# A long convolution by nine block products instead of ten, with the sums for it on POOL

## The chip, the cores and the metric

The kernel runs on one core of a Trainium2 chip. The core has a matrix engine (TensorE, PE in the profile, with its weight loads as PEld), a vector engine (DVE), a scalar engine (ACT), a general engine (POOL) and a queue that issues transfers (SP); POOL issues indirect transfers of its own. Each engine works through its own instructions in a fixed order and waits on semaphores for the others. The metric is the device time of one execution in microseconds (us), the median of several runs. Four runs of the kernel before took 3074.35, 3076.90, 3073.13 and 3070.82 us, with a median of 3073.74 us.

## The reference, cut to what matters

The program is two layers of a network (a convolution with gates, a mixture of experts, an attention, a feed-forward part). The change concerns the first of them alone, for `x` of shape (16, 256, 512) and a context `ctx` of the same shape:

```python
vr  = v.reshape(B, 32, 8, 512)              # v = layernorm(x); x2 = x1 = ctx
kv  = vr[:, :, :, None, :] * x2r[:, :, None, :, :]        # B, 32, i, j, 512
y   = irfft(rfft(kv, 1024) * rfft(k, 1024))[..., :512]    # causal convolution, one filter k[h] per h
y   = y + kv * skip
out = einsum('bhijl,bhil->bhjl', y, x1r)
```

So for each of 32 filters (h), 16 batches and 8 x 8 pairs (i, j), a sequence of 512 products is convolved with a filter of 512 taps, weighed by the context and summed over i. The first expert layer that follows uses weights `w1` and `w2` of eight experts, 4 MB each.

## The kernel before, in words

The convolution is done as matrix products with a Toeplitz matrix. The 512 positions are cut into four blocks of 128. Write x0 to x3 for the four blocks of `kv`, and T0 to T3 for the four 128x128 blocks of the Toeplitz matrix of one filter (`ut`, loaded per filter from `in_kt`). Then block l of the result is the sum over m up to l of T(l-m) x(m): one product for block 0, two for block 1, three for block 2 and four for block 3, ten in all. Each product has 128x128 weights and 512 columns, and the profile counts two passes for each in fp32.

The loop of `conv_shared` (L744) runs over the 32 filters h. A step h has two halves of eight batches, so that 8 batches x 64 pairs give the 512 columns. `conv` (L283) does one half: for each block lc, the products on PE (L292), then on DVE the weighing by the context (L297, out of PSUM into `pr`) and the sum over i (L304, into one block of `oT`), and then one of the four products `kv` of the half after it (`product`, L274, on DVE). `extra` puts small pieces of other work between them. Around the two halves of a step stand, in this order on PE: the transposes of the step before (`norm2_turned`), the list `mid`, the turning of the next step's inputs (`turn_inputs`: `pvt`, `pt`, `psk`, L256 to L262), half 1, the keys (`keys`, L211), the list `end`, and four transposes of `oT` (`after_conv`, L316, tile `po`), one for each block. DVE then adds `po` to `xt` (L317), and statistics on DVE (L78, L80), four small operations on POOL (L82 to L86) and one on ACT (L91) make the normalized rows `xh`. `begin(h + 2)` does the same statistics for the inputs of a later step, between the keys and `end`.

`mid` and `end` carry the shared expert and the router of the four steps before, and differ with q = h % 4, so that four steps make a group:

- q = 0: `mid` holds one `outs` (L503) and the router's `parts` (L396); `end` holds a short `whole` (L407).
- q = 1: `mid` one `hidden` (L490), `end` `rank_rows` and one `hidden`; the router's `tops` lies between the blocks on DVE, and its exponential (L439) on ACT in half 1.
- q = 2: `mid` one `hidden`, `end` one `hidden`; here POOL sends twelve indirect transfers of a group in a row (L371 to `xgd`, L1910 to `rtok`).
- q = 3: `mid` one `outs`, `end` two; each `outs` ends in an addition on DVE (L507).

In steps 3 to 18 `ranks` (L663, L667, L668, on DVE, and two indirect transfers to `tokd` on POOL) stands behind `end` and ahead of `after_conv`; steps 0, 2 and 22 have other pieces of the sorting there.

What sets the order: PE, DVE and ACT keep the order in which the code is written (`manual_schedule`, L743). POOL's and SP's order is chosen by the scheduler when the kernel is built and then fixed. Three PSUM buffers `y` take turns (`ps_y`), `pvt` has one, `kv` two, `ut` two, `ct` three. The expert weights are loaded one quarter per step by SP from step 2 on, four quarters of `w1` and then four of `w2` (`load_experts`, L339, the last one in step 9); the first product with `w2` comes after the loop (L914).

Of the kernel before, what the change touches and what calls it, by code (L numbers as in the profile page):

```python
# [42 lines left out]
class Kernel:  # L43
# [59 lines left out]
    def conv_shared(self, x1d, xgd):  # L103
        nc, tc, a = self.nc, self.tc, self.a
        with ExitStack() as ctx:
# [136 lines left out]
            def begin(h):  # L242

                xt, ct, ut = loaded.pop(h)
                vh = hp.tile([P, D], F32, tag="vh", name="vh")
                self.normalized(vh, xt, self.stats(xt, small))
                return {"h": h, "xt": xt, "ct": ct, "ut": ut, "vh": vh, "kv": {}}

            def skipped(c):

# [2 lines left out]
                nc.vector.scalar_tensor_tensor(z, c["vh"], skip[:, h : h + 1], c["ct"], ALU.mult, ALU.mult)  # L253

            def turn_inputs(c):
                c["vt"] = vt = ps_v.tile([P, DC, P], F32, tag="v", name="pvt")  # L256
                for k in range(DC):
                    nc.tensor.transpose(vt[:, k, :], c["vh"][:, k * P : (k + 1) * P], self.ident)
# [10 lines left out]
            def product(c, half, mc):  # L269

                cols = slice(half * 64, half * 64 + 64)
                if mc == 0:
                    c["kv"][half] = hp.tile([P, DC, hb * NH * NH], F32, tag="kv", name="kv")
                nc.vector.tensor_tensor(  # L274
                    c["kv"][half][:, mc, :].rearrange("p (b j i) -> p b j i", i=NH, j=NH),
                    c["vt"][:, mc, cols].rearrange("p (b i) -> p b i", i=NH)
                    .unsqueeze(2).to_broadcast([P, hb, NH, NH]),
                    c["cT"][:, mc, cols].rearrange("p (b j) -> p b j", j=NH)
                    .unsqueeze(3).to_broadcast([P, hb, NH, NH]),
                    ALU.mult,  # L280
                )

            def conv(c, half, nxt, extra):  # L283

                cols = slice(half * 64, half * 64 + 64)
                if half == 0:
                    c["oT"] = hp.tile([P, DC, P], F32, tag="oT", name="oT")
                kv, ut, cT = c["kv"].pop(half), c["ut"], c["cT"]
                for lc in range(DC):
                    y = ps_y.tile([P, hb * NH * NH], F32, tag="y", name="y")  # L290
                    for mc in range(lc + 1):
                        c["conv"] = nc.tensor.matmul(  # L292
                            y, ut[:, (lc - mc) * P : (lc - mc + 1) * P], kv[:, mc, :],
                            start=(mc == 0), stop=(mc == lc),
                        ).ins
                    pr = hp.tile([P, hb, NH, NH], F32, tag="pr", name="pr")
                    nc.vector.tensor_tensor(  # L297
                        pr,
                        y.rearrange("p (b j i) -> p b j i", i=NH, j=NH),
                        cT[:, lc, cols].rearrange("p (b i) -> p b i", i=NH)  # L300
                        .unsqueeze(2).to_broadcast([P, hb, NH, NH]),
                        ALU.mult,
                    )
                    nc.vector.tensor_reduce(  # L304
                        c["oT"][:, lc, cols].rearrange("p (b j) -> p b j", j=NH), pr, AX.X, ALU.add
                    )
                    if nxt is not None:
                        product(*nxt, lc)
                    for f in extra.get(lc, []):
                        f()  # L310

            def after_conv(c):
                xt = c["xt"]
                po = ps_t.tile([P, DC, P], F32, tag="t", name="po")
                for lc in range(DC):
# [23 lines left out]
            def load_experts(c):  # L339
                if c < DC:  # L340
                    nc.sync.dma_start(
                        self.e_w1[:, c].rearrange("p (e h) -> p e h", h=EH),
                        a["w1"].rearrange("e (c p) h -> c p e h", p=P)[c],
                    )
                else:
                    c -= DC
                    n = E * EH // P // 4
                    nc.sync.dma_start(
                        self.e_w2.rearrange("p (f d) -> p f d", d=D)[:, n * c : n * c + n, :],
                        a["w2"].rearrange("e (c p) d -> p (e c) d", p=P)[:, n * c : n * c + n, :],  # L350
                    )

            xhs = []

# [388 lines left out]
            with tc.manual_schedule(engines=order):  # L743
                for h in range(HC):  # L744
# [9 lines left out]
                    with tc.issue_after(last_load[0]):  # L754
                        if w is None:
                            w = load_shared_weights()
                        if 2 <= h < 2 + DC + 4:
                            load_experts(h - 2)
                    now["w"] = w
                    now["xt"].append(c["xt"])  # L760
# [59 lines left out]
                    if last:  # L820
                        with tc.issue_after(self.normed):
                            for t in range(T4 - 1):
                                send(now["r"], t)
                    turn = (now["xT"], h)
            norm2_turned(*turn)
            r = logits(now, T4 - 1, 1)
            for f in tops(r):
# [12 lines left out]
                send_route(r, 0)  # L840
            for t in range(T4):
                outs(now, t)


    def routed(self, xgd, ygd, early):
# [1241 lines left out]
```

## Time and profile before

| what | value |
|---|---|
| median of four runs | 3073.74 us (3070.82 to 3076.90) |
| the profiled execution: time, span | 3076.3 us, 3074.6 us |
| PE busy, share of the span | 3002.9 us, 98% |
| DVE, ACT, POOL busy | 1434.3, 661.7, 923.1 us |
| from 35 to 960 us (the convolution): PE, DVE, ACT, POOL busy of 925 us | 900.64, 677.73, 148.14, 291.37 us |
| the Toeplitz products, L292 (1280 passes, all in the convolution) | 565.7 us |

Times in the profile are microseconds from the span's start. A group's row gives the line, the engine, the operation, the tiles out and in, the number of instructions, the busy time and the mean of one in ns, and then the idle time of that engine just before them with what ended it. Matmuls overlap, so 1280 passes with a mean of 592 to 597 ns each start 0.429 us apart (20 passes of one half from 493.80 to 502.38 us). In a timeline a row gives the start, the duration and the instruction; brackets hold the idle time before it and what released it. A chain of waits names who waited for whom, the sum, the number of times and the longest.

### The profile page before, as it was taken

How to read it: one execution, taken by the hardware profiler on the slowest of the kernel's cores; microseconds unless marked ns; L12 is line 12 of the kernel's file. 1: busy time of each engine (PE TensorE's matmuls, PEld its weight loads, DVE VectorE, ACT ScalarE, POOL GpSimd, SP SyncE). 2: the span in 40 equal slices, each digit the busy share in tenths (PEclk: the TensorE clock that was granted, in tenths of full speed). 3: DMA queues.
4: the chain of work that ended last, by engine and by line, in shares of the span. 5: the costliest groups of instructions: out<-in, count | busy, mean ns of one | idle time of the engine just before them, and what ended most of it. 6: DMA issues, size and time to landing. Idle time of an engine off the chain costs nothing.

```text
span 3074.6 us, 34728 instructions
## 1 busy us (share of the span) xinstructions
PE 3002.9 (98%) x12825; PEld 1529.8 (50%) x12825; DVE 1434.3 (47%) x2652; ACT 661.7 (22%) x1250; POOL 923.1 (30%) x1270
## 2 busy tenths in 40 slices
PE   8999999999999999889999999999999999999998
PEld 4444444445455666554554554454444444444443
DVE  6777777777664434443433333443333232222222
ACT  1111111111111111243333323324121111111110
POOL 2233333232223200165545555534110300301201
PEclk9999999999999999989999999999999999999999
DMA  4232211211215653311211221212120100100100
GB/s 118 70 104 88 63 60 56 71 57 60 59 39 182 204 168 129 109 55 46 87 52 52 76 64 47 69 53 69 59 103 28 55 14 14 55 10 11 45 0 29
DMA packets 119218, 209.87 MB, mean 68 GB/s; under 512 B 27592, under 2 KB 47976, under 8 KB 118400
## 3 DMA queue, kind: packets, MB, share of 16 engines
q1 hardware_dynamic: 90752, 125.63, 13.4%
q0 software_dynamic: 28288, 81.92, 8.2%
q8 instruction: 105, 1.72, 0.2%
q14 instruction: 73, 0.60, 0.1%
HBM read 140.12 MB, written 67.37 MB: 67 GB/s over the span
## 4 chain that ended last, share of the span: by engine, by line
PE 85%; DVE 6%; issue 5%; POOL 3%; DMA 1%; ACT 0%; SPq 0%; POOLq 0%; DVEq 0%; ACTq 0%
PE y L292 15%; PE po L1879 14%; PE ph L1821 13%; PE po L1625 9%; PE phg L895 4%; PE pog L914 4%; PE pqn L1504 3%; PE pout L503 3%; PE ph L490 3%; PE pqr L1501 2%; PE pqn L1512 2%; PE pt L99 2%; PE pqr L1508 1%; DVE pr L297 1%; PE ptg L884 1%
## 5 line engine op out<-in xcount | busy, mean ns | idle before, releaser
L292 PE MATMUL y<-kv,ut 128*128 128x512 f32 x1280 | 565.7, 597 | 0.6 <-DVE pr L297 0.6
L1625 PE MATMUL po<-nw,w 128*128 128x512 f32 x1024 | 445.7, 593 | 0.0
L1879 PE MATMUL po<-p,ht 128*128 128x512 f32 x1024 | 445.1, 592 | 0.0
L292 PEld LDWEIGHTS y<-kv,ut 128*128 128x128 f32 x1280 | 243.2, 192 | 297.3 <-issue 287.1
L1625 PEld LDWEIGHTS po<-nw,w 128*128 128x128 f32 x1024 | 192.0, 190 | 235.1 <-issue 229.6
L1879 PEld LDWEIGHTS po<-p,ht 128*128 128x128 f32 x1024 | 192.7, 190 | 233.4 <-issue 232.0
L1821 PE MATMUL ph<-w,w 128*128 128x512 f32 x640 | 281.2, 592 | 0.0
L297 DVE TENSOR_TENSOR pr<-y,cT 128x512 f32<-128x512 f32 x256 | 174.5, 682 | 145.2 <-PE y L292 145.1
L1883 DVE TENSOR_TENSOR res<-res,po 128x512 f32<-128x512 f32 x128 | 87.7, 685 | 315.5 <-PE po L1879 315.5
L1821 PEld LDWEIGHTS ph<-w,w 128*128 128x128 f32 x640 | 121.5, 190 | 152.6 <-issue 152.6
L304 DVE TENSOR_REDUCE oT<-pr 128x64 f32<-128x512 f32 x256 | 175.6, 686 | 8.8
L274 DVE TENSOR_TENSOR kv<-pvt,cT 128x512 f32<-128x512 f32 x256 | 173.9, 680 | 0.0
L1919 POOL DMA_INDIRECT gw<-kvd,keys_of x128 | 133.5, 1043 | 49.8 <-issue 37.8
L267 POOL TENSOR_TENSOR xt<-xt,sk 128x512 f32<-128x512 f32 x32 | 40.8, 1274 | 339.8 <-DVE sk L266 281.9
L1519 DVE TENSOR_TENSOR w<-pqr,w 128x512 f32<-128x512 f32 (+1 forms) x72 | 45.4, 631 | 202.7 <-ACT sw L1517 189.0
L895 PE MATMUL phg<-w,xTg 128*128 x568 | 134.5, 380 | 0.6 <-issue 0.5
L914 PE MATMUL pog<-w,hT 128*128 x284 | 133.6, 593 | 0.0
L1504 PE MATMUL pqn<-w,m 128*128 128x512 f32 (+1 forms) x288 | 116.9, 548 | 7.2 <-ACT kn L1537 7.2
L490 PE MATMUL ph<-xT,w_s 128*128 128x512 f32 x256 | 117.5, 603 | 0.0
L1821 PE MATMUL ph<-xT,w 128*128 128x512 f32 x256 | 116.4, 592 | 0.0
L503 PE MATMUL pout<-w_s,ht 128*128 128x512 f32 x256 | 115.3, 600 | 0.0
L1835 ACT ACTIVATE ht<-ht,p1b 128x512 f32<-128x512 f32 x96 | 69.3, 722 | 212.9 <-DVE ht L1840 212.9
(291 smaller groups left out, 3771.8 us busy)
## 6 DMA issues: line engine op xcount, KB each, us to landing
xg<-xgd SPq DMA_DIRECT2D x71, 256.0 KB, 2.8
ygd<-y SPq DMA_DIRECT2D x71, 256.0 KB, 2.0
xt<-in_x_dram SPq DMA_DIRECT2D x32, 256.0 KB, 3.4
ct<-in_ctx_dram SPq DMA_DIRECT2D x32, 256.0 KB, 3.3
ut<-in_kt_dram SPq DMA_DIRECT2D x32, 256.0 KB, 2.6
w<-in_w_dram SPq DMA_DIRECT2D x8, 1024.0 KB, 5.3
x1d<-xt SPq DMA_DIRECT2D x32, 256.0 KB, 2.9
x3s<-xt POOLq DMA_DIRECT2D x32, 256.0 KB, 2.8
```

The lines of the kernel that those rows point to most:

```text
L274: nc.vector.tensor_tensor(c["kv"][half][:, mc, :].rearrange("p (b j i) -> p b j i", i=NH, j=NH), c["vt"][:, mc, cols].rearrange("p (b i) - ...
L292: c["conv"] = nc.tensor.matmul(y, ut[:, (lc - mc) * P : (lc - mc + 1) * P], kv[:, mc, :], start=(mc == 0), stop=(mc == lc),).ins
L297: nc.vector.tensor_tensor(pr, y.rearrange("p (b j i) -> p b j i", i=NH, j=NH), cT[:, lc, cols].rearrange("p (b i) -> p b i", i=NH) .unsque ...
L304: nc.vector.tensor_reduce(c["oT"][:, lc, cols].rearrange("p (b j) -> p b j", j=NH), pr, AX.X, ALU.add)
L490: nc.tensor.matmul(ph, w["sw1"][:, c, f * P : (f + 1) * P], xT[:, c, :], start=(c == 0), stop=(c == DC - 1),)
L503: nc.tensor.matmul(po, st["ht"][f][:, tok], w["sw2"][:, f, :], start=(f == 0), stop=(f == NC_ - 1))
L895: nc.tensor.matmul(ph, xT[:, c, :], w1[:, c, bass.ds(e * EH, EH)], start=(c == 0), stop=(c == DC - 1))
L914: nc.tensor.matmul(po, hT[:, q, :], w2[:, bass.ds(e * (EH * D // P) + q * D, D)], start=(q == 0), stop=(q == EH // P - 1),)
L1504: nc.tensor.matmul(pqn[k][i], m0[:, 2 * hp + i, :], q0, start=True, stop=False)
L1625: nc.tensor.matmul(po, ut[:, n].rearrange("p a j q -> p (a j q)"), nw[:, 2 * hp + i, :], start=(n == 0), stop=(n == HEADS - 1),)
L1821: nc.tensor.matmul(ph, w[:, c, :], x[:, c, :], start=(start and c == 0), stop=(c == half - 1), skip_group_check=True,)
L1879: nc.tensor.matmul(po, ht[f, i // T4][:, toks], w2[:, f, :], start=(f == fs[0]), stop=(f == fs[-1]))
```

## The change

Block 2 and block 3 share a product. With s = x0 + x1,

- block 2 = T2 s + (T1 - T2) x1 + T0 x2
- block 3 = T2 s + (T3 - T2) x0 + T1 x2 + T0 x3

which is nine products, where T2 s counts once. New work makes the operands and takes the shared product apart:

- `differences`: two 128x128 subtractions on POOL per step, T1 - T2 and T3 - T2 (`dt`).
- in `product`, once two of the four blocks of a half are there, one 128x512 addition on POOL (`x01`, the sum s).
- in `conv`, the product T2 s goes to a PSUM buffer `m`; ACT copies it to SBUF (`both`); three products of block 3 go to a `y` buffer; DVE adds them onto `both`; POOL multiplies `both` by the context (before, DVE did this for all four blocks). Then two more products add onto `m` for block 2, and DVE weighs and sums block 2 as before. The sum over i of block 3, on DVE, is kept back as `late`: it stands after block 1's sum of the next half, or, for half 1, at the head of `after_conv`.
- the order of a half is now block 0, block 1, T2 s, block 3, the rest of block 2. `y` has two PSUM buffers and `m` one.
- `sums`, `twice` (`both`) and `diffs` lie in the last quarter of `w2`'s place in SBUF; so the load of this quarter is moved from step 9 to behind the loop (`load_second(3)`).

```diff
             def turn_inputs(c):
+                differences(c)
...
+                if mc == 1:
+                    c["sum"][half] = x01 = sums[half]
+                    nc.gpsimd.tensor_tensor(x01, c["kv"][half][:, 0, :], c["kv"][half][:, 1, :], ALU.add)
+            mixed = lambda lo, n: self.e_w2[:, E * EH * D // P - lo - n : E * EH * D // P - lo]
+            sums, twice, diffs = [mixed(i * D, D) for i in range(2)], mixed(2 * D, D), [
+                mixed(3 * D + i * 2 * P, 2 * P).rearrange("p (i x) -> p i x", i=2) for i in range(2)
+            ]
+            def differences(c):
+                c["dt"] = dt = diffs[c["h"] % 2]
+                ut = c["ut"].rearrange("p (d x) -> p d x", x=P)
+                for i in range(2):
+                    nc.gpsimd.tensor_tensor(dt[:, i, :], ut[:, 2 * i + 1, :], ut[:, 2, :], ALU.subtract)
...
-                for lc in range(DC):
-                    y = ps_y.tile([P, hb * NH * NH], F32, tag="y", name="y")
-                    for mc in range(lc + 1):
-                        c["conv"] = nc.tensor.matmul(
-                            y, ut[:, (lc - mc) * P : (lc - mc + 1) * P], kv[:, mc, :],
...
+                products(y, [(T[0], x[0])])
+                weighed(0, y)
+                if nxt is not None:
+                    product(*nxt, 0)
+                beside(0)
+                y = block("y", 2)
+                products(y, [(T[1], x[0]), (T[0], x[1])])
+                weighed(1, y)
+                if "late" in c:
+                    c.pop("late")()
+                for k in (1, 2):
+                    if nxt is not None:
+                        product(*nxt, k)
+                    beside(k)
+                y2 = block("m", 1)
+                products(y2, [(T[2], x01)])
+                both = twice
+                nc.scalar.copy(both, y2)
+                y = block("y", 2)
+                products(y, [(dt[:, 1, :], x[0]), (T[1], x[2]), (T[0], x[3])])
+                nc.vector.tensor_tensor(both, both, y, ALU.add)
+                nc.gpsimd.tensor_tensor(by_i(both), by_i(both), ctx_(3), ALU.mult)
+                if nxt is not None:
+                    product(*nxt, 3)
+                beside(3)
+                products(y2, [(dt[:, 0, :], x[1]), (T[0], x[2])], start=False)
+                weighed(2, y2)
+                c["late"] = lambda: summed(3, by_i(both))
 
             def after_conv(c):
+                c.pop("late")()
                 xt = c["xt"]
...
-                        if 2 <= h < 2 + DC + 4:
+                        if 2 <= h < 2 + DC + 3:
                             load_experts(h - 2)
...
                     turn = (now["xT"], h)
+            self.load_second(3)
             norm2_turned(*turn)
```

`weighed(lc, y)` is the weighing out of PSUM followed by `summed`, the sum over i; `beside(k)` runs the small pieces that stood behind block k.

More of the change, by code (lines that the diff above doesn't have):

```diff
@@ L246, in begin @@
                 self.normalized(vh, xt, self.stats(xt, small))
-                return {"h": h, "xt": xt, "ct": ct, "ut": ut, "vh": vh, "kv": {}}
+                return {"h": h, "xt": xt, "ct": ct, "ut": ut, "vh": vh, "kv": {}, "sum": {}}
             def skipped(c):
@@ L288, in conv, with products, summed @@
                 kv, ut, cT = c["kv"].pop(half), c["ut"], c["cT"]
-                for lc in range(DC):
-                    y = ps_y.tile([P, hb * NH * NH], F32, tag="y", name="y")
-                    for mc in range(lc + 1):
+                x01, dt = c["sum"].pop(half), c["dt"]
+                T = [ut[:, d * P : (d + 1) * P] for d in range(DC)]
+                x = [kv[:, m, :] for m in range(DC)]
+                by_i = lambda t: t.rearrange("p (b j i) -> p b j i", i=NH, j=NH)
+                ctx_ = lambda lc: (
+                    cT[:, lc, cols].rearrange("p (b i) -> p b i", i=NH).unsqueeze(2).to_broadcast([P, hb, NH, NH])
+                )
+                def products(y, terms, start=True, stop=True):
+                    for k, (t, v) in enumerate(terms):
                         c["conv"] = nc.tensor.matmul(
-                            y, ut[:, (lc - mc) * P : (lc - mc + 1) * P], kv[:, mc, :],
-                            start=(mc == 0), stop=(mc == lc),
+                            y, t, v, start=(start and k == 0), stop=(k == len(terms) - 1), skip_group_check=True
                         ).ins
[L296 to L303, printed above, removed]
+                def summed(lc, pr):
                     nc.vector.tensor_reduce(
@@ L306, in conv, with weighed, beside @@
                     )
-                    if nxt is not None:
-                        product(*nxt, lc)
-                    for f in extra.get(lc, []):
-                        f()
+                def weighed(lc, y):
+                    pr = hp.tile([P, hb, NH, NH], F32, tag="pr", name="pr")
+                    nc.vector.tensor_tensor(pr, by_i(y), ctx_(lc), ALU.mult)
+                    summed(lc, pr)
+                def beside(k):
+                    for f in extra.get(k, []):
+                        f()
+                block = lambda tag, bufs: ps_y.tile([P, hb * NH * NH], F32, tag=tag, name=tag, bufs=bufs)
+                y = block("y", 2)
[10 more added lines that the diff above has]
+                for k in (1, 2):
+                    if nxt is not None:
+                        product(*nxt, k)
[4 more added lines that the diff above has]
+                nc.scalar.copy(both, y2)
+                y = block("y", 2)
+                products(y, [(dt[:, 1, :], x[0]), (T[1], x[2]), (T[0], x[3])])
[7 more added lines that the diff above has]
+                c["late"] = lambda: summed(3, by_i(both))
             def after_conv(c):
+                c.pop("late")()
                 xt = c["xt"]
@@ L345, in load_experts @@
                 else:
[L346 to L351, printed above, removed]
+                    self.load_second(c - DC)
             xhs = []
@@ L842, in conv_shared, with load_second @@
                 outs(now, t)
+    def load_second(self, c):
+        n = E * EH // P // 4
+        self.nc.sync.dma_start(
+            self.e_w2.rearrange("p (f d) -> p f d", d=D)[:, n * c : n * c + n, :],
+            self.a["w2"].rearrange("e (c p) d -> p (e c) d", p=P)[:, n * c : n * c + n, :],
+        )
     def routed(self, xgd, ygd, early):
```

## The prediction

> **What bounds the kernel now.** First the page: span, engines, the group of the changed line.
>
> ```profile
> span 3074.6 us, 34728 instructions
> ...
> PE 3002.9 (98%) x12825; PEld 1529.8 (50%) x12825; DVE 1434.3 (47%) x2652; ACT 661.7 (22%) x1250; POOL 923.1 (30%) x1270
> ...
> L292 PE MATMUL y<-kv,ut 128*128 128x512 f32 x1280 | 565.7, 597 | 0.6 <-DVE pr L297 0.6
> ...
> L267 POOL TENSOR_TENSOR xt<-xt,sk 128x512 f32<-128x512 f32 x32 | 40.8, 1274 | 339.8 <-DVE sk L266 281.9
> ```
>
> PE is the bound, and its Toeplitz passes waited 0.6 us in all: each pass removed is time, unless PE must wait where it didn't. Next PE's chain of waits up to 1000 us, whose first row is nearly all of it:
>
> ```profile
> PE pvt L258 <- DVE kv L274: 17.2, 11, 3.6
> ```
>
> Then the end of a half 1, where the change puts a DVE sum ahead of PE's transposes: the timelines of DVE and PE at step 16 (q = 0).
>
> ```profile
> 493.33 0.64 PE L316 MATMUL po<-ident,oT 128*128 128x128 f32 x4
> ```
>
> ```profile
> 492.14 0.69 DVE L304 TENSOR_REDUCE oT<-pr 128x64 f32<-128x512 f32 x1
> 492.75 0.68 DVE L274 TENSOR_TENSOR kv<-pvt,cT 128x512 f32<-128x512 f32 x1
> 493.34 0.68 DVE L78 BATCH_NORM_STATS2 ln_st<-xt 128x6 f32<-128x512 f32 x1
> 494.13 0.18 DVE L80 BATCH_NORM_AGGREGATE ln_mv<-ln_st 128x2 f32<-128x6 f32 x1
> 494.23 0.77 DVE L663 TENSOR_TENSOR cmp<-o_krow,o_key 128x512 f32<-128x512 f32 x1
> 495.03 0.69 DVE L667 TENSOR_REDUCE o_rank<-cmp 128x2 f32<-128x512 f32 x1
> 495.75 0.23 DVE L668 TENSOR_SCALAR o_where<-o_rank,o_batch 128x2 int32<-128x2 f32 x1
> 495.89 0.68 DVE L317 TENSOR_TENSOR xt<-xt,po 128x512 f32<-128x512 f32 x1
> ```
>
> PE transposes `oT` at 493.33 because its last sum ended at 492.83; DVE comes to `after_conv` only at 495.89. That lag costs nothing today. Last, POOL in step 18 (q = 2), where twelve indirect transfers, 1.275 us apart, fill it:
>
> ```profile
> 529.59 1.04 POOL L371 DMA_INDIRECT xgd<-xh,slots  x1 [1.56 <-DVE slots L466]
> ...
> 543.73 0.97 POOL L1910 DMA_INDIRECT rtok<-rt,o_where  x1 [0.30 <-issue]
> 544.71 1.30 POOL L267 TENSOR_TENSOR xt<-xt,sk 128x512 f32<-128x512 f32 x1
> 549.03 0.32 POOL L216 TENSOR_TENSOR kr<-kr,tab 128x64 f32<-128x64 f32 x1 [3.02 <-ACT kr L215]
> ```
>
> **A. Removed: 64 products.** 64 halves x 2 passes x 0.429 us (20 passes from 493.80 to 502.38) = -54.9 us, all on PE's path.
>
> **B. Removed: PE's waits for `kv`.** `pvt` waits for the fourth `kv` of half 0. That product now stands ahead of block 2's weighing and sum, and DVE starts closer behind PE (see C): in step 17 DVE would end it about 11.4 us after PE's transposes, and PE arrive at 12.0. I take all 17.2 us: -17.2.
>
> **Work beside.** DVE keeps 12 operations of 0.68 us per half (the addition onto `both` takes the place of one weighing). ACT gains a copy, 0.586 us (a 128x512 copy out of PSUM, L100) x 64 = 37.5 us; POOL 128 operations of 1.27 us and 64 of 0.455 us (L225, 128x128), 192 us on 291 of 925. On average there is room; what counts is who waits.
>
> **C. Added: the late sum ahead of `po`.** DVE reaches it after `begin`'s statistics, `end`'s additions and `ranks`. In half 1 DVE's new list is about as long as PE's 7.72 us, so block 2's weighing starts right behind PE, as the last one did before; only the `kv` product (0.60 us from start to start) is no longer behind it, and the late sum (0.69) comes in. So the sum ends about where L317 could start today, + 0.1 us. The first three transposes don't wait, which gives back 3 x 0.11. From each step's rows: q = 0 with `ranks` (4, 8, 12, 16) 2.4 us each, without (20, 24, 28) 0.8; q = 3, where L507 waits for PE first and the 0.69 comes in full, 2.8 with `ranks` (7, 11, 15) and 1.25 without (19, 23, 27); q = 1 none (PE is busy longer); steps 1, 2, 3: 1.5, 4.0, 3.2; step 31: 1.1. In q = 2 it is POOL that is late: in the order as built, the sum s of half 1 and both context products lie among and behind the twelve transfers: 529.6 + 12 x 1.275 + 4 x 1.27 + 1.3 = 551.3 less the last gap 0.3 = 551.0; late sum 551.1 to 551.8; PE arrives at 550.1: 1.4 x 7. Sum: 9.7 + 2.3 + 8.5 + 3.7 + 8.8 + 1.1 + 9.9 = +44.0 us. DVE's queue behind it (L317, statistics) moves with it.
>
> **D. Added: PE waits for ACT's copy** before block 2's last two products, 6.0 us into a half. The copy stands behind what ACT still holds. q = 1, half 1: behind the exponential.
>
> ```profile
> 515.60 0.15 DVE L438 TENSOR_TENSOR ex<-m,m 128x4 f32<-128x4 f32 x1
> ```
>
> That half began at 510.10; with the late sum ahead, `ex` leaves DVE 6.2 us into the half, ACT's 0.21 and 0.59 follow: PE goes on at 7.2: 1.2 x 7 = 8.4. The half 0 behind a q = 2 step with `ranks`: POOL, free at 551.0, does keys, statistics, both differences (0.91 more) and two `tokd` transfers before `xh`; ACT's `xh` ends near 560.0, the copy at 560.6, PE wants it at 551.9 + 0.4 + 6.0 = 558.3: 2.35 x 4 = 9.4. Behind a q = 0 step with `ranks`: 0.65 x 4 = 2.6. Elsewhere the copy is in time. Sum +20.4.
>
> **E. The start.** POOL's first difference waits for `ut`, ahead of the first `vh`, which PE waits for (8.50 us): two of 0.455 and a wait for the load, together 0.9 to 2.5; I take +1.8.
>
> **F. Restarts.** No row shows a pass behind a wait inside a group; between 0 (weights already in) and 0.19 us (the L292 weight load). 39 waits come and 11 go: 0 to 5.3; I take 5.3, since at `pvt` the weight loads waited too.
>
> **G. The clock.** After the 1.89 us pause ending at 390.28 the granted clock fell; after an equal one in step 17 it didn't:
>
> ```profile
> 389.00:394.00 5.00, 3.72 (x12) 2.14 (x13) 1.22 (x2) 1.98 (x3) 0.00 (x0) 0.75 0.01 3
> 505.00:510.00 5.00, 3.11 (x14) 1.67 (x13) 3.05 (x10) 1.25 (x2) 0.00 (x0) 1.00 0.00 0
> ```
>
> (the fraction behind POOL's count is the clock). It cost 1.7 us (step 13 took 32.23 us, others of its kind 30.54); the 3.59 us pause in step 3 cost 3.2. So one pause in five near 1.9 us trips it, a long one surely. Of my new pauses of 2.3 us and more I let nine half-rate stretches follow: 9 x 1.7 = 15.3, less 4.9 that go, less 2.0 where a slow PE waits less in D: +8.4; bounds -4.9 and +25. The Trainium skill ("TensorE: Matmul & The Clock Gate", HAM oscillation) warns only of idle gaps above some 3.4 us; by it one or two of mine would trip, G would be an estimated -2, and the sum some 10 us lower; the 1.89 us row speaks against it.
>
> **The moved load.** One 1 MB transfer (0.43 us on SP, 5.3 us to land) leaves step 9, where nobody waited, and stands behind the loop after an `x1d` store near 936 us; `e_b` and two stores queue behind it. The first product with `w2` is at 977: 0, covered by 35 us; without that cover 5.3 and the store ahead.
>
> **Sum.** -54.9 - 17.2 + 44.0 + 20.4 + 1.8 + 5.3 + 8.4 = +7.8 on the profiled 3076.3 us gives 3084.1. That run stands 2.6 above the median, so 3081.5 us, 0.25% slower.
>
> **Unknown prices.** POOL's context product reads an operand with repeats: 1.27 (L267, plain, same size) to 1.82 us (four times L225, which repeats). POOL's rows of 32, 64 and 128 elements (253, 321, 455 ns) lie on one line, which gives 1.26 at 512: 1.27 taken; 1.82 adds some 12 us in q = 2. Sharing between POOL and DVE: none to see in 513.90 to 515.17, where DVE kept 0.69 and 0.68; 0 taken. ACT's copy 0.59 to 0.81 (L91).
>
> **The rivals.**
> 1. *Faster: the late sum is not waited for* (chance 0.17). If DVE gains on PE inside half 1, it reaches the sum before PE reaches the fourth transpose, and C falls, with half of F and G: 3081.5 - 44 - 7 = 3030, and up to 3062 where only the waits under 2 us vanish. Deciding point: DVE 2.5 us earlier at step 16's 495.89. For: PE leaves DVE idle 145 us before L297. Against: that idle time lies inside the halves, while the eight rows above run without a gap.
> 2. *POOL binds in more steps* (0.15): its products take 1.8 us or wait behind its transfers. C and D grow by 12 to 25: 3094 to 3107. Against: 484 of 925 us busy.
> 3. *Every new pause of a microsecond or more trips the clock* (0.08): 25 stretches, G +37 at most: 3098 to 3110.
> 4. *The late load collides* with `e_b` and the expert rows (0.05): 5 to 10 us, 3087 to 3092.
>
> **How the numbers follow.** My case has 0.55, with a range of 3064 to 3098 (D and C each a third off). Within it I put 0.28 slower, 0.17 the same, 0.10 faster; 0.2% (6 us) is about what this kernel's runs can tell from nothing. Rival 1 is faster; 2, 3 and 4 slower, but for 0.01. Faster 0.27, same 0.18, slower 0.55. The range of 8 in 10 leaves out two thirds of rival 1 and the top of 2 and 3: 3052 to 3106.
>
> **What would show it.** L292's successor with 1152 passes near 509 us and 0.429 us apart (A); no `pvt` wait on `kv` (B); a new first row, `po` waiting for DVE `oT`, 24 times and near 44 us, longest near 4 (C); block 2's passes waiting for ACT, 15 times and 20 us (D); more stretches under full clock before 960 us (G). It is wrong if `po` waits under 20 us, or if POOL's 128x512 operations run above 1.4 us.

## The result, and the profile after

The changed kernel takes 3077.12 us (median of 40 runs, 3074.86 to 3085.31), the kernel before 3072.93 us (60 runs, 3068.97 to 3077.07). The ratio is 1.0016, with a 95% interval of 1.0011 to 1.0020: 0.16% slower, which is less than the 0.2% that I had called the limit of what can be told from nothing; with this many runs the interval leaves out 1 all the same. The forecast was 3081.5 us. The two profiled executions are even: 3076.3 us before and 3076.26 us after, spans 3074.6 and 3074.5 us. The accounts below are made between these two. That the medians stand 4.2 us apart is within what single executions differ by, and one profile of each can't say where those 4 us lie.

From here on a mark in the trace divides the kernel: the first transposes of the expert layer (`ptg`) behind the convolution. They start at 970.16 us before and at 968.86 us after. So the convolution became 1.3 us shorter, and what follows took 2104.4 us before and 2105.6 us after. 128 passes less on PE had been worth 54.9 us, and next to nothing of it is left. The question is where it went.

The page of the kernel after, first the engines, then a part of the group of the convolution's passes:

```profile
span 3074.5 us, 34937 instructions
...
PE 2966.2 (96%) x12697; PEld 1504.9 (49%) x12697; DVE 1448.0 (47%) x2652; ACT 694.6 (23%) x1314; POOL 1117.5 (36%) x1462
...
L321 PE MATMUL y<-kv,ut 128*128 128x512 f32 x640 | 307.8, 613 | 0.0
```

PE has exactly 128 instructions less than the 12825 of before and is busy 36.7 us less, in a span of the same length: it stands idle instead. PE's chain of waits up to 1000 us says for whom (who waited for whom, the sum in us, how often, the longest):

```profile
PE po L375 <- DVE oT L326: 38.0, 22, 3.9
PE m L321 <- ACT w L358: 7.0, 11, 0.8
PE pt L99 <- DMA ct<-in_ctx_dram: 5.8, 1, 5.8
PE pwide L767 <- DVE o_tmp L757: 3.6, 1, 3.6
PE pt L99 <- ACT xh L91: 3.6, 1, 3.6
PE pvt L259 <- ACT vh L91: 2.5, 1, 2.5
```

The row of before, `pvt` waiting 17.2 us for `kv`, is gone. In its place stand `po`, waiting for the late sum, and `m`, waiting for ACT's copy. (The wait for `ct` is the kernel's start, and was there before under another name.) Two more losses have no row. One is the clock. In the windows below (columns: length, then busy time and count of PE, weight loads, DVE, ACT and POOL, then the granted clock as a fraction, the DMA share and GB/s) it falls behind a pause:

```profile
340.00:345.00 5.00, 3.61 (x11) 1.53 (x9) 2.22 (x4) 0.81 (x1) 0.07 (x1) 1.00 0.25 63
345.00:350.00 5.00, 3.76 (x6) 1.81 (x7) 4.22 (x9) 0.13 (x1) 3.16 (x6) 0.66 0.49 153
```

0.66 over 5 us is 1.7 us lost (the trace's stretches at half rate last 3.41 us, some of them twice that). Summed over all windows of 5 us from 30 to 960 us, the clock takes 10.2 us before (six times 3.41 us) and 17.0 us after (ten). The other is hidden in half 1 of every step. The timeline of the kernel after in step 20 (start, duration, instruction; in brackets the idle time before it and what released it):

```profile
602.82 1.88 PE L321 MATMUL y<-kv,ut 128*128 128x512 f32 x4
603.42 0.68 DVE L326 TENSOR_REDUCE oT<-w 128x64 f32<-128x512 f32 x1
604.19 0.59 ACT L358 COPY w<-m 128x512 f32<-128x512 f32 x1 [5.74 <-DVE oT L326]
604.83 1.12 PE L321 MATMUL m<-kv,w 128*128 128x512 f32 x2
```

Four passes that start 0.43 us apart from 602.82 would let the next start at 604.54; it starts at 604.83, and the second of it 0.1 us late again. The profile puts no wait there, since the modelled end of the pass before covers most of the gap. A half 1 takes 8.12 us in place of 18 x 0.429 = 7.72, in 24 steps; in the seven with q = 1 it takes 8.83, of which 0.84 have a row and 0.27 have none; only in step 31 is there nothing. What ACT waited for in step 20 is the late sum of half 0 on DVE: there is one buffer for `both`, and the copy of half 1 may not overwrite it until the late sum of half 0 has read it. That makes 24 x 0.40 = 9.6 us, a term that the prediction doesn't have. The 1.11 us of q = 1 have another cause, the exponential of term D (experiments 3 and 9 tell the two apart).

### The profile page after: what moved, and what is told of

It reads as the page before. It is cut to its first block, busy times and chain, and to the rows that moved or that the text cites. A ratio compares the mean times of both kernels' runs of the same rounds, so it can differ in the third digit from the quotient of the medians.

```text
span 3074.5 us, 34937 instructions
## 1 busy us (share of the span) xinstructions
PE 2966.2 (96%) x12697; PEld 1504.9 (49%) x12697; DVE 1448.0 (47%) x2652; ACT 694.6 (23%) x1314; POOL 1117.5 (36%) x1462
## 4 chain that ended last, share of the span: by engine, by line
PE 84%; DVE 7%; POOL 3%; issue 3%; DMA 1%; ACT 1%; SPq 0%; POOLq 0%; ACTq 0%; DVEq 0%
PE po L1942 14%; PE po L1688 13%; PE ph L1884 12%; PE y L321 7%; PE m L321 5%; PE phg L958 4%; PE pog L977 4%; PE pout L557 4%; PE pqn L1567 3%; PE ph L544 3%; DVE oT L326 2%; PE pqr L1564 2%; PE pt L99 2%; PE pqn L1575 2%; DVE pr L332 1%
## 5 line engine op out<-in xcount | busy, mean ns | idle before, releaser
L321 PE MATMUL y<-kv,ut 128*128 128x512 f32 x640 | 307.8, 613 | 0.0
L321 PEld LDWEIGHTS y<-kv,ut 128*128 128x128 f32 x640 | 124.4, 199 | 145.5 <-issue 144.7
L326 DVE TENSOR_REDUCE oT<-pr 128x64 f32<-128x512 f32 x192 | 131.7, 686 | 6.6
L70 POOL TENSOR_TENSOR ln_rs<-ln_mv,eps 128x1 f32<-128x1 f32 x64 | 12.8, 200 | 316.6 <-DVE ln_mv L68 315.9
L332 DVE TENSOR_TENSOR pr<-y,cT 128x512 f32<-128x512 f32 x128 | 87.0, 680 | 85.6 <-PE y L321 85.2
L285 POOL TENSOR_TENSOR w<-kv 128x512 f32<-128x512 f32 x64 | 92.0, 1437 | 88.7 <-DVE kv L275 68.7
```

What stands on the lines that cost most here:

```text
L321: c["conv"] = nc.tensor.matmul(y, t, v, start=(start and k == 0), stop=(k == len(terms) - 1), skip_group_check=True).ins
L326: nc.vector.tensor_reduce(c["oT"][:, lc, cols].rearrange("p (b j) -> p b j", j=NH), pr, AX.X, ALU.add)
```

## The experiments

Experiments 1 to 4 ran on a chip on which the kernel before took 3074.81 us; 5 to 8 and 9 to 10 ran on chips on which it took 3110.84 and 3110.68 us. There the part behind the convolution is some 35 us longer, and the convolution is as long as elsewhere (`ptg` at 968.63 us with the load moved alone). So times are compared as ratios to the kernel before on the same chip, and convolutions by `ptg`. "Clock" is the time lost to a lower clock, counted as above; waits are those from 35 to 968 us.

| kernel | median us | ratio to before (95%) | `ptg` at | `po` waits | `m` waits | clock |
|---|---|---|---|---|---|---|
| before | 3072.93 | 1 | 970.16 | 0 | 0 | 10.2 |
| after | 3077.12 | 1.0016 (1.0011 to 1.0020) | 968.86 | 38.0 | 7.0 | 17.0 |
| before, late sum alone | 3104.06 | 1.0092 (1.0075 to 1.0109) | 997.34 | 28.1 | 0 | 17.0 |
| after, `cmp` in another form | 3075.99 | 1.0004 (0.9994 to 1.0013) | 965.53 | 36.4 | 6.2 | 17.1 |
| after, late sum early | 3065.14 | 0.9965 (0.9952 to 0.9977) | 963.00 | 14.4 | 16.5 | 18.8 |
| + copy early | 3058.57 | 0.9940 (0.9924 to 0.9957) | 951.58 | 14.3 | 11.3 | 11.9 |
| before, load moved alone | 3110.19 | 0.9993 (0.9984 to 1.0003) | 968.63 | 0 | 0 | 8.6 |
| + `ranks` in DVE's gap | 3078.47 | 0.9903 (0.9887 to 0.9920) | 937.88 | 18.1 | 0 | 17.1 |
| + q = 2 on DVE | 3069.19 | 0.9880 (0.9862 to 0.9897) | 921.85 | 1.1 | 9.8 | 6.8 |
| after, two buffers `both` | 3109.36 | 1.0009 (0.9997 to 1.0022) | 964.86 | 40.9 | 10.0 | 15.4 |
| + two buffers `both` | 3058.54 | 0.9834 (0.9818 to 0.9850) | 915.06 | 1.5 | 10.6 | 10.2 |
| + no `ranks` in q = 2 | 3045.61 | 0.9791 (0.9775 to 0.9807) | 902.01 | 1.5 | 0.6 | 5.1 |

A line with + contains the line with + above it, down to "after, late sum early"; no kernel of the table leaves work out. `ptg`, waits and clock are those of the one profiled execution. That of "after, late sum early" was the slowest of its six, 9 us above their median.

**1. The late sum alone, with ten products** (term C by itself):

```diff
-                    nc.vector.tensor_reduce(...)        # the last sum of a half
+                    total = lambda lc=lc, pr=pr: nc.vector.tensor_reduce(...)
+                    if half == 1 and lc == DC - 1:
+                        c["late"] = total
+                    else:
+                        total()
             def after_conv(c):
+                c.pop("late")()
```

> The kernel before, with its ten products, in which only the last sum over i of half 1 is held back and put at the head of after_conv, as the change does: term C alone, with nothing added on POOL or ACT. Theory: po waits for DVE's oT some 20 times, 25-34 us; part of the waits of pvt for kv goes (up to 10 us); the time is 3092-3102 us. Rival (the waits at po are made by POOL's new work, not by the place of the sum): po waits under 8 us and the time stays at 3070-3078 us.

Measured: 0.92% slower, which is 29 us and 2 us above the range. PE's chain of waits:

```profile
PE po L321 <- DVE oT L304: 28.1, 16, 3.9
PE pvt L258 <- DVE kv L274: 5.0, 3, 1.7
```

28.1 us come at `po`, 12.2 us go at `pvt`, and the clock takes 6.8 us more: 22.7 of the 27.2 us by which `ptg` moved. So the place of the sum makes these waits by itself, without any new work on POOL or ACT. The waits by kind are those of the kernel after: 2.03 us in q = 0 with `ranks` and 2.63 in q = 3 with `ranks`. None stands in q = 2 but for step 2 and a wait of 0.46 in step 22 that is not for the sum, so there the kernel after must wait for another reason.

**2. The late sum moved forward**, in the kernel after:

```diff
                     conv(c, 1, (nxt, 0) if nxt is not None else None, two)
+                    if q != 2:
+                        c.pop("late")()
                     keys(c)
```

> The changed kernel, with the late sum of half 1 put directly behind block 2's sum, ahead of the keys, the statistics of begin and the ranks, in all steps but those with q = 2. Theory (the late sum's place ahead of po is what eats the gain): the waits of po for oT fall from 38.0 us to 10-15 us, all in steps with q = 2; with fewer restarts and two to four half-rate stretches fewer the time is 3045-3052 us. Some waits of pvt for kv may come back, up to 5 us. Rival (POOL's extra work and its sharing with DVE are what cost): the waits move elsewhere and the time stays at 3070 us or above.

The waits at `po` went to 14.4 us, as the theory had it, but the time only to 3065.14 us, 13 us above its range. PE's chain of waits from 35 to 968 us:

```profile
PE m L321 <- ACT w L358: 16.5, 15, 2.4
PE po L376 <- DVE oT L326: 14.4, 9, 3.9
PE y L321 <- DVE pr L332: 6.0, 8, 0.9
```

Of the 23.6 us gained at `po`, 9.5 come back in the half 0 behind it at `m`, and 6.0 at `y`, because DVE and ACT are as late as ever: with `po` no longer holding PE up, PE meets their lag one stage later. The new waits of `m`, up to 2.4 us, stand in steps 4, 5, 9, 13 and 17, in the half 0 behind steps with `ranks`. Behind q = 0 I had put 0.65 us each; 0.65 and the 2.03 of the vanished wait make 2.7, and 1.8 + 0.75 (at `y`) came. Theory and rival were both half right: the place of the sum costs, and most of its price is a lag that moves on.

**3. The copy moved ahead of the exponential**, besides:

```diff
-                for k in (1, 2):
-                    if nxt is not None:
-                        product(*nxt, k)
-                    beside(k)
                 y2 = block("m", 1)
                 products(y2, [(T[2], x01)])
                 both = twice
                 nc.scalar.copy(both, y2)
+                for k in (1, 2):
+                    if nxt is not None:
+                        product(*nxt, k)
+                    beside(k)
```

> The kernel with the late sum of half 1 moved forward, and besides that the product T2 s and ACT's copy of it written ahead of the products kv 1 and 2 and what stands beside blocks 1 and 2, so that on ACT the copy stands before the router's exponential. Theory (block 2's last passes wait for the copy because it stands behind the exponential): the waits of m for ACT fall from 7.0 us to under 1 us, and the time by 7-9 us against the kernel with the late sum moved alone, to 3037-3044 us. Rival (the copy is late because the sum s or the product T2 s is late): the 7 us stay and the time is that of the kernel with the late sum moved alone.

The seven waits of 0.84 us in half 1 of q = 1 are gone, with 6.6 us in time (3065.14 to 3058.57), near the 7 to 9 us expected from one to the other; D's first part had the right cause. By their lengths these halves lost 1.11 us each and now lose 0.40 like the others, by the one buffer, so the move gives 7 x 0.71 = 5.0 us there. (`ptg` moves by 11.4 us, 6.8 of them by the clock.) The sum of the `m` waits is 11.3 us and not under 1 us, since the waits of the experiment before, in half 0, remain.

**4. `cmp` in another form.** In steps with q = 2 and `ranks`, `po` waits 2.15 to 2.21 us in the kernel after. Its timeline in step 18 shows why, and it isn't POOL's lateness that I had forecast:

```profile
545.82 1.28 POOL L268 TENSOR_TENSOR xt<-xt,sk 128x512 f32<-128x512 f32 x1
546.88 3.25 DVE L717 TENSOR_TENSOR cmp<-o_krow,o_key 128x512 f32<-128x512 f32 x1
547.04 1.28 POOL L285 TENSOR_TENSOR w<-kv 128x512 f32<-128x512 f32 x1
548.26 1.27 POOL L362 TENSOR_TENSOR w<-w,cT 128x512 f32<-128x512 f32 x1
...
549.49 0.82 POOL L216 TENSOR_TENSOR kr<-kr,tab 128x64 f32<-128x64 f32 x1
...
551.20 0.67 DVE L326 TENSOR_REDUCE oT<-w 128x64 f32<-128x512 f32 x1
...
551.93 0.33 PE L375 MATMUL po<-ident,oT 128*128 128x128 f32 x1 [2.17 <-DVE oT L326]
```

POOL had the context product (L362) ready at 549.53, in time. But DVE's `cmp`, which took 0.84 us in these steps before (0.68 where nothing of POOL's lay beside it), took 3.25 us. It came when POOL was in the first of three 128x512 operations in a row, and ends 0.6 us after the third, as if it had run only then. The rest of `ranks` and the late sum stand behind it on DVE. `cmp` reads two tensors from SBUF. The experiment gave it one:

```diff
-                nc.vector.tensor_tensor(
-                    cmp, krow.unsqueeze(1).to_broadcast([P, 2, S]),
-                    key[:, hs].unsqueeze(2).to_broadcast([P, 2, S]), ALU.is_lt,
-                )
+                for i in range(2):
+                    nc.vector.tensor_scalar(
+                        cmp[:, i, :], krow, key[:, 2 * q + i : 2 * q + i + 1], None, ALU.is_lt,
+                    )
```

> The changed kernel, with the comparison cmp of ranks done by two tensor_scalar operations (128x256, one tensor from SBUF and one value per partition) in place of one tensor_tensor with two tensors from SBUF. Theory (in steps with q = 2 cmp is stretched to 3.25 us by POOL's 128x512 operations beside it): the two operations take 1.0 us or less together also beside POOL, po's waits in the four steps with q = 2 and ranks fall from 2.15-2.2 us to 0.8 us or less and in all from 38.0 to 29-33 us; the half 0 behind them then starts earlier and its wait for ACT's copy, which I had forecast at 2.35 us each, comes up in part, so that the time is 3068-3076 us. Rival (POOL's context product is late by itself): po's waits in these steps stay at 1.4 us or more and are put down to POOL's chain; or the new operations are stretched as well: 3076-3080 us.

The rival holds: nothing is won (1.0004; `po` waits 1.95 to 1.98 us in these steps). The timeline of this kernel in step 18:

```profile
541.65 1.29 POOL L268 TENSOR_TENSOR xt<-xt,sk 128x512 f32<-128x512 f32 x1
542.69 3.20 DVE L718 TENSOR_SCALAR cmp<-o_krow,o_key 128x256 f32<-128x256 f32 x2
542.87 1.28 POOL L285 TENSOR_TENSOR w<-kv 128x512 f32<-128x512 f32 x1
544.10 1.28 POOL L362 TENSOR_TENSOR w<-w,cT 128x512 f32<-128x512 f32 x1
```

Elsewhere the two operations take 0.32 to 0.35 us each. Here the first took 2.88 us, from 542.69 to 545.57, past the end of POOL's third operation at 545.38, and the second 0.40 us behind it. So two tensors are not needed for it.

**5. POOL operations set beside `cmp`**, in the kernel before (the load of `w2`'s last quarter moved to make room; the additions and copies write idle space only):

```diff
+                if q % 4 != 1:
+                    nc.vector.tensor_copy(idle[:, 0:1], key[:, 0:1])
+                    for i in range(1 if q % 4 == 3 else 4):
+                        src = idle[:, 0:D]
+                        if q % 4 == 2:
+                            nc.gpsimd.tensor_copy(idle[:, 2 * D : 3 * D], src)
+                        else:
+                            nc.gpsimd.tensor_tensor(idle[:, 2 * D : 3 * D], src, idle[:, D : 2 * D], ALU.add)
                 nc.vector.tensor_tensor(cmp, ...)
```

> The kernel before, with the load of w2's last quarter moved behind the loop, and idle POOL operations of 128x512 set beside cmp: four additions of two tensors in ranks 0, 4, 8, 12, none in ranks 1, 5, ..., four copies (one tensor) in ranks 2, 6, ..., one addition in ranks 3, 7, .... They write idle space only. Theory (DVE's operation with two tensors from SBUF waits until POOL's operations with two tensors, back to back, are through): cmp takes 4 to 5.5 us beside four additions, 1.5 to 2.1 us beside one, and 0.8 us beside none; the reduction with one tensor keeps 0.69 us. Open is what four copies do: 0.8 us if two tensors on POOL are needed for it. Rival (cmp was long for another reason, such as POOL's transfers): cmp keeps 0.8 us everywhere.

A miss, and a telling one: `cmp` kept 0.68 to 0.80 us everywhere. (The kernel ran once, in 3120.37 us against 3110.84 for the kernel before on that chip, which gives no verdict on its time.) The timeline in the first `ranks`, beside four additions:

```profile
115.44 0.80 DVE L674 TENSOR_TENSOR cmp<-o_krow,o_key 128x512 f32<-128x512 f32 x1
115.64 0.64 POOL L82 TENSOR_TENSOR ln_rs<-ln_mv,eps 128x1 f32<-128x1 f32 x1
116.24 1.26 POOL L673 TENSOR_TENSOR w<-w 128x512 f32<-128x512 f32 x1
116.27 0.69 DVE L678 TENSOR_REDUCE o_rank<-cmp 128x2 f32<-128x512 f32 x1
116.99 0.54 DVE L679 TENSOR_SCALAR o_where<-o_rank,o_batch 128x2 int32<-128x2 f32 x1
```

`cmp` came first, and POOL was the one that waited: L82 on a single column, 0.19 us by itself, took 0.64 and ended with `cmp`, and the addition started only then. Beside that addition the reduction kept its 0.69 us, and `o_where`, 0.23 us by itself, took 0.54 and ended when the addition did (117.50). So it is not a sharing but a taking of turns: one goes through, the other stands. What decides the turn is shown only in part. In step 18 above `cmp` came while POOL was in L268, and stood until POOL's whole row was through. Here too POOL was in an operation when `cmp` began (L225, 128x128, 115.23 to 115.68), and yet `cmp` went ahead of L82. What the four copies do to `cmp` stays open, since they too came after it. The Trainium skill ("SBUF — State Buffer", Who interferes with whom) describes this as an exclusive lock that goes to whoever issues first, for a whole instruction; the rows here agree that the other stands for a whole instruction, but in step 18 above DVE stood through three of POOL's in a row, not one.

**6. The moved load alone**, in the kernel before:

```diff
-                        if 2 <= h < 2 + DC + 4:
+                        if 2 <= h < 2 + DC + 3:
                             load_experts(h - 2)
...
+            load_experts(DC + 3)
             norm2_turned(*turn)
```

> The kernel before with the moved load alone: the last quarter of w2 is loaded behind the loop in place of step 9. Theory: nobody waits for it, 3071-3077 us. Rival (the late load collides with the transfers at the loop's end): 3078-3086 us, with a wait of the first expert products for w2.

0.9993 (0.9984 to 1.0003): the load costs nothing, and rival 4 of the prediction falls. (The times in the expectation were for the first chip; the ratio is what counts.)

**7. `ranks` in DVE's gap**, on top of experiment 3. DVE stands idle for some 3.2 us ahead of half 1 in most steps, and its long list is behind half 1:

```diff
+                    if 3 <= h < 3 + HC // 2:
+                        ranks(h - 3)
                     conv(c, 1, (nxt, 0) if nxt is not None else None, two)
```

> The kernel with late sum and copy moved forward, and besides that ranks taken from its place ahead of after_conv and put right ahead of half 1, where DVE stands idle for some 3.2 us in each step (3.23 us ahead of L332 at 502.61 in the run before this). Theory (DVE's list behind half 1 is the cause: once po does not wait for it, DVE carries its lag into the next half 0, where y waits for DVE and block 2's passes for ACT's copy, which stands behind xh): the waits of y for DVE fall from 6.0 us to under 1 us, those of m for ACT from 11.3 to under 4 us, those of po from 14.3 to 8-10 us, since cmp no longer runs beside POOL's products in q = 2; time 3034-3044 us. Rival (POOL's longer list makes xh and the copy late): the waits of m for ACT stay at 9 us or more and are put down to POOL's ln_nb, and the time is 3050 us or above.

The lag was DVE's: the waits at `y` and at `m` are all gone (6.0 and 11.3 us), and the ratio falls from 0.9940 to 0.9903. But `po` in q = 2 with `ranks` now waits 3.06 to 3.15 us, where the expected sum left about one. The timeline of step 18:

```profile
519.96 0.97 POOL L1976 DMA_INDIRECT tokd<-o_vals,o_where  x1 [0.30 <-issue]
521.24 0.97 POOL L1976 DMA_INDIRECT tokd<-o_vals,o_where  x1 [0.30 <-issue]
...
525.92 1.29 POOL L362 TENSOR_TENSOR w<-w,cT 128x512 f32<-128x512 f32 x1
...
527.25 0.69 DVE L326 TENSOR_REDUCE oT<-w 128x64 f32<-128x512 f32 x1 [5.20 <-POOL w L362]
527.99 0.48 PE L376 MATMUL po<-ident,oT 128*128 128x128 f32 x1 [3.15 <-DVE oT L326]
```

Moving `ranks` forward moved its two transfers to `tokd` forward as well, into POOL's row of transfers and ahead of the context product: 2 x 1.275 = 2.55 us. DVE waits 5.20 us for POOL. That is a POOL lateness of the kind that the prediction had put into the kernel after; here 2.55 of the 3.1 us come from the two transfers that this edit moved.

**8. The product of q = 2 on DVE**, on top:

```diff
-                nc.gpsimd.tensor_tensor(by_i(both), by_i(both), ctx_(3), ALU.mult)
+                on = nc.vector if half == 1 and c["h"] % T4 == 2 else nc.gpsimd
+                on.tensor_tensor(by_i(both), by_i(both), ctx_(3), ALU.mult)
...
-                    if q != 2:
-                        c.pop("late")()
+                    c.pop("late")()
```

> As the kernel with ranks in the gap, and in half 1 of the steps with q = 2 the context product of block 3 done on DVE in place of POOL, with the late sum moved forward there as well. Theory (in q = 2 the late sum waits for POOL, which is behind its twelve transfers): the remaining po waits of q = 2 go but for step 2's 3.9 us, some 4-7 us of time against the kernel with ranks in the gap. Rival: DVE's two-tensor product waits for POOL's sum of x0 and x1 in its turn, takes 2 us or more, and block 2's weighing behind it is late: no gain, or a loss of up to 5 us.

`ptg` moves 16 us forward, 10 of them by the clock, and the ratio falls to 0.9880, 7 us of time (the profiled execution took 3064.51 us, 4.7 less than its median, the one before it 1.3 more than its own). PE's chain of waits from 35 to 968 us begins with:

```profile
PE m L321 <- ACT w L354: 9.8, 4, 5.1
```

These four stand in the half 0 behind steps 6, 10, 14 and 18 (1.55, 1.62, 1.55 and 5.13 us), the four places where term D had 2.35 us each. The first three come as D had it, by POOL's late statistics, `xh` and ACT's copy behind it. In the kernel after no more than 0.34 us stood at any of the four places, because PE had already waited 2.2 us at `po`. The fourth is longer for another reason. Its statistics stand on POOL behind the differences, and these wait for the load of `ut`:

```profile
520.65 0.87 POOL L303 TENSOR_TENSOR w<-ut 128x128 f32<-128x128 f32 x2 [3.57 <-DMA ut<-in_kt_dram]
```

So the sum of 9.8 lies near D's 9.4 by chance. (The wait of 3.9 us at `po` in step 2 went as well; 1.8 us at `y` came in step 3.)

**9. Two buffers for `both`**, once in the kernel after and once on top of experiment 8 (the third quarter of `w2` is then loaded behind the loop too):

```diff
-            sums, twice, diffs = [mixed(i * D, D) for i in range(2)], mixed(2 * D, D), [
+            sums, twice, diffs = [mixed(i * D, D) for i in range(2)], [mixed(i * D, D) for i in (2, 4)], [
...
-                both = twice
+                both = twice[half]
```

> The changed kernel with two buffers for both in place of one (the second lies in the third quarter of w2, whose load goes behind the loop too). In the run of the changed kernel ACT's copy in half 1 stands until DVE's late sum of half 0 has read the one buffer (5.74 us ahead of L358 at 604.19), and block 2's last products start 0.40 us late in every half 1, a wait too short for a row of its own. Theory: this gap of 0.40 us goes in all 31 halves 1 in which it stands, but in the steps where PE then waits at po for the late sum it comes back there; so po's waits rise by 5-9 us to 43-47 us and the time falls by only 2-6 us, to a ratio of 0.9995-1.0010 to the kernel before. The waits of m for ACT in q = 1, which stand behind the exponential, stay near 6 us. Rival (the copy waits for something else): the 0.40 us stay and nothing changes.

> The same second buffer for both in the kernel with late sum and copy forward, ranks in the gap and q = 2's product on DVE. Here PE doesn't wait at po, so nothing gives the gap back. Theory: 31 x 0.40 = 12 us less than that kernel, a ratio of 0.9835-0.9855 to the kernel before (that one had 0.988). Rival: DVE's late sum or POOL's product is then what block 2 waits for, and less than 5 us are gained.

In the kernel after, the 0.40 us go from all 24 halves 1 (the seven with q = 1 keep their 1.11, which is thus the exponential's), `po` waits 2.9 us and `m` 3.0 us longer, and the time hardly moves: 1.0009 (0.9997 to 1.0022) against 1.0016. Without the waits at `po` the same edit takes the 0.40 us from all 31 halves 1, and brings the ratio from 0.9880 to 0.9834, 14 us of 3110 (`ptg` moves by 6.8 us only, with 3.4 more lost to the clock). So the 0.40 us were real, their cause is the one buffer, and in the kernel after they hide ahead of other waits.

**10. No `ranks` in q = 2**, on top: two in steps 5, 9 and 13, the last one in step 19.

```diff
-                    if 3 <= h < 3 + HC // 2:
-                        ranks(h - 3)
+                    for k in at.get(h, []):      # 1 per step from 3 on, 0 where q = 2, 2 where q = 1
+                        ranks(k)
```

> The kernel with the second buffer, and besides no ranks in steps with q = 2 (two in steps 5, 9 and 13, the last one in step 19), so that their two transfers don't stand in POOL's queue behind the twelve. Theory: in the half 0 behind such a step xh and with it ACT's copy are late because of POOL (waits of m for ACT of 1.55, 1.62, 1.55 and 5.13 us in steps 7, 11, 15 and 19 of the kernel with q = 2's product on DVE); they shrink by up to 2.55 us each (two transfers of 1.275) to under 1 us in steps 7, 11 and 15, and with the clock some 5-9 us go: a ratio 0.002-0.003 below the kernel with the second buffer. Rival (two ranks in one gap of 3.2 us make half 1 of q = 1 late): y or po waits for DVE there, 1 us in three steps.

More than expected: 0.9791, which is 0.0043 less. All four waits at `m` went, the 4.96 us of step 19 too; a single one of 0.58 us is new, in step 18, where the differences wait 1.98 us for `ut`. PE's chain of waits from 35 to 968 us is now:

```profile
PE pwide L769 <- DVE o_tmp L759: 3.2, 1, 3.2
PE pkey L679 <- DVE o_by_tok L677: 2.7, 1, 2.7
PE pt L99 <- ACT xh L91: 2.1, 1, 2.1
PE y L321 <- DVE pr L332: 1.8, 1, 1.8
PE po L377 <- DVE oT L326: 1.5, 4, 0.7
```

`ptg` stands at 902.01 us, 68 us ahead of the kernel before, and A + B are 72. 5.1 of the 68 are the clock's. So nearly all that A + B had promised can be had; the kernel after lost it to the order and the buffers of the work around the nine products. This version is 2.1% faster than the kernel before (0.9775 to 0.9807) and so faster than the change as made. What the same moves would do for the kernel before, with its ten products, was not run. Its PE waited 17.2 us for DVE at `pvt`, and that part of the 72 might be had without the nine.

## Why the prediction was right, and where it was not

The forecast lay 4.4 us above the median, with "slower" as the likeliest and a change so small that it can hardly be told. It came out by terms of which some were wrong, and offset each other. Each against the profiled executions:

| term | predicted | measured | from |
|---|---|---|---|
| A, 128 passes | -54.9 | -54.9 | 18 passes of a half 0 in 7.73 us, 20 in 8.58 before |
| B, `pvt` for `kv` | -17.2 | -17.2 | the row is gone |
| C, `po` for the late sum | +44.0, 24 times | +38.0, 22 times | its row |
| D, block 2 for the copy | +20.4, 15 times | +7.0, 11 times; +3.9 with no row | its row; lengths of the halves |
| (no term) copy for the buffer `both` | 0 | +9.6 | 24 halves 1 of 8.12 us |
| E, start | +1.8 | +0.9 | first Toeplitz pass at 13.08, before at 12.20 |
| F, restarts | +5.3 | +1.1 | what is left over |
| G, clock | +8.4 | +6.8 | ten stretches, six before |
| (no term) `pwide`, `xh`, `pkey`, `y` | 0 | +3.3, +1.5, -0.7, -0.6 | their rows, before and after |
| sum, up to `ptg` | +7.8 | -1.3 | |

- **A and B** are right, and the last experiment shows that they can be had nearly in full. The sign for A, a busy time near 509 us for 1152 passes, came 18 us higher: 527.3 us, with overlaps counted once. The rows of L321 add up to more (573 us), because the passes now form several groups and the overlapping ends of each are counted.
- **C** has the right mechanism and is 6 us too large. q = 0 came with 2.03 and 0.42 us (2.4 and 0.8 forecast), q = 3 with 2.63 and 1.05 (2.8 and 1.25), steps 1, 2, 3 with 1.06, 3.93, 2.67 (1.5, 4.0, 3.2), step 31 with none. The step "in q = 2 it is POOL that is late" failed: with `ranks` 2.15 to 2.21 us came, because `cmp` stood behind POOL's three operations (read from the timelines: no run takes this away alone), and without `ranks` 0.6 us in two steps (1.4 x 7 forecast). The context product itself was ready at 549.53 in step 18, not at 551.0. That goes back to "sharing between POOL and DVE: none to see, 0 taken". The stretch I had looked at, 513.90 to 515.17, held DVE operations that don't meet POOL. The sign that I had named for it, POOL operations above 1.4 us, came (L285 took 1.437 us on average), but the loss was on DVE, in `cmp`, where I had named none.
- **D** was mis-sized, and its sentence "Elsewhere the copy is in time" is wrong. I had asked what stands ahead of the copy on ACT, and not who still reads the buffer that it writes. Of the 9.4 us behind q = 2 only 1.8 came, since they and q = 2's wait in C are one delay: PE cannot wait twice for the same lag. I had added them as if both were paid; experiment 8, with C's part taken away, gave 4.7 in three of the four places, and in the fourth 5.1 for another reason. The 8.4 of q = 1 came as 7 x 1.11 = 7.8, the 2.6 behind q = 0 as 0.9, and 0.5 came behind step 3. So D itself is 10.9 us. With the buffer's 9.6 the copy costs 20.5 us, so the size of D is right by chance alone.
- **G** is near. In the kernel after, the pause at `po` trips the clock in two of eight waits of 2.03 to 2.21 us, in three of four of 2.63 to 2.67, and in the one of 3.93; the other four of the ten stretches lie at the waits at `pwide` and for `xh`, 3.6 us each. In the kernel of experiment 1 a stretch came at all nine `po` waits of 2.03 us and more, four of them of 2.03, so the length of a pause does not settle it alone. The Trainium skill's gap of some 3.4 us ("TensorE: Matmul & The Clock Gate", HAM oscillation), by which G would have been an estimated -2, doesn't hold here; the row at 389 us of the kernel before was the better guide.
- **F** is not measured; it is what the other rows leave: 1.1 us, nearer to its lower bound of 0, where I took the upper.
- **The moved load** costs nothing, shown alone in experiment 6. POOL's operand with repeats costs nothing either: L362 takes 1.274 us like L267's plain one, so the upper value of 1.82 us falls.
- **Rival 1**, that the late sum is not waited for, was wrong for this kernel: experiment 1 shows the wait by itself. But its size was wrong as well: taking the wait away (experiment 2) gave some 16 us by the ratios and not 44 + 7, because the lag comes back one stage later. **Rival 2**, POOL binds in more steps, fell for the kernel after; POOL's lateness shows only in later kernels, as the 3.1 us waits of experiment 7 and the first three of experiment 8. **Rival 3** fell, since 11 of the 17 `po` waits of 1 us and more in the kernel after left the clock alone. **Rival 4** fell.

## What to carry to other kernels

When work is taken from the engine that binds, list for each stage who is late next, and don't add up waits that stem from one lag: taking away the first only lets the next one show, and only when the lag itself is moved into an idle gap does the gain arrive. For each new instruction ask three things: what stands ahead of it on its engine, who still reads the buffer that it writes, and which instruction of DVE or POOL runs at the same moment. A gap of 0.4 us that has no row in the chain of waits is found by holding the length of a repeated stage against its count of instructions.

## What the runs showed of the hardware

- DVE and POOL take turns on some operations. DVE's comparison of two tensors from SBUF, 0.68 us by itself, took 3.25 us when it met three 128x512 POOL operations in a row: it came 1.06 us into the first and ran behind the third. With one tensor and a value per partition it waited as well (2.88 us for an operation that takes 0.32 to 0.35 elsewhere). When POOL came to a single column while the comparison ran, POOL waited: 0.64 us for what takes 0.19. A reduction on DVE beside a POOL addition kept 0.69 us.
- A drop of the granted clock cost 1.7 us each time, or twice that (3.41 or 6.83 us at half rate). `po` waits of 2.03 us were joined by one in one case of four in the kernel after, and in all four in that of experiment 1.
- POOL's indirect transfers take a fixed place in its queue, 1.275 us each, and moving one comparison on DVE to the other side of half 1 moved two of them ahead of a product that PE was waiting for.
